# Layer 0, second MLP of a four-layer graph network: the input added inside it, sums on GpSimd, output blocks between all chunks, earlier degrees, and shorter rare branches

## The chip, the cores and the metric

The kernel runs on one core of a Trainium2 chip, as one launch. The metric is the device time of the whole program in microseconds (us). The program is a long one: some 33,600 instructions over four layers, and the change touches mostly one part of the first layer, some 340 us long, and four branches elsewhere.

## The reference

There are T = 1250 nodes with D = 512 features, and 20,000 directed edges (`src`, `dst`). Each of four layers adds to x a graph convolution and a mixer, and then a feed-forward part with experts. Layer 0 is the one that matters here:

```python
edge_index = jnp.stack([src, dst])
xn = _layernorm(x, axis=-1)
x = x + _L0_gnn_ref(xn, edge_index, ...) + _L0_mix_ref(xn[None], ...)[0]
x = x + _L0_ffn_ref(_layernorm(x, axis=-1)[None], ...)[0]

def _L0_gnn_ref(x, edge_index, W, b):          # with a loop at every node
    deg = segment_sum(ones, row); dis = rsqrt(deg)
    h = x @ W.T + b
    return relu(segment_sum((dis[row] * dis[col])[:, None] * h[row], col))

def _L0_mix_ref(x, ...):                       # two layers of attention + MLP
    for i in range(2):
        ...                                    # attention on layernorm(x), added to x
        y = layernorm(x, ln2_g[i], ln2_b[i])
        h = gelu(y @ W1[i] + b1[i])            # 512 -> 2048
        x = x + h @ W2[i] + b2[i]              # 2048 -> 512
    return x
```

## The kernel before

**Layout.** The nodes are ten tiles of 125 rows. A tensor with nodes on partitions is `[125, 10, 512]`; transposed tensors (`yT`, `hT`) have features on partitions, and the nodes are then cut into three chunks of 500, 500 and 250 columns (`CH`). All of it is in 32-bit floats. Every matmul group goes through `mm` (L187), or through L1181 in the products described next. PSUM results are taken by DVE or ACT; `add_to` (L213) adds a PSUM result into a tile on DVE. The scheduler keeps an engine's instructions in an order that follows the program's; `tc.keep_in_program_order` and `pinned` fix an instruction or a load at its place.

**The MLP of layer 0.** `l0_mlp(i, ...)` runs over four units u (512 hidden features each) and, within a unit, over the three chunks. A product of two matrices is made as seven products of quarter blocks (`seven`) in place of eight: before it, sums and differences of the quarters are formed, by `left_sums` (L1163 to L1166) and `right_sums` (L1170 to L1173), and while it runs, intermediate results are copied out of PSUM to `p` by ACT (L1185), combined on DVE (L1194, L1195), and added to the outputs. `hidden` makes `hT` of one chunk from `yT`, the first weights and `tx`, the sums of the chunk's quarters of `yT`. `outputs` makes the output rows of one chunk from `hT` and the second weights, two node tiles (a block) at a time, and adds each quarter into `xm` (which is `xn` here) on DVE: L1311 adds an earlier result out of SBUF, L213 one out of PSUM. In unit 1 the bias `b2` is added to each finished tile (L1328).

The first MLP is called with `roomy=True`: `tx` has room for all chunks and is made once. The second MLP, the one of the change, is not roomy, because the graph's tensors need space. There `tx` is a single buffer that is made anew on DVE for every chunk of every unit, as soon as the hidden products before it are done with it. The order of its blocks is written out: hidden of chunk 0, hidden of chunk 1, outputs of chunk 0, hidden of chunk 2, outputs of chunk 1, outputs of chunk 2, and then the next unit.

**Work aside.** After each of the twelve chunks, the second MLP calls `aside()`, which runs one piece of the generator `steps()`: five pieces with two calls of `graph.arrived(t)`, five with the scaling of two tiles of `hs` by `dis` and its division into two parts (`parted`, L678 and L679), and then `graph.degrees()`. The graph is a matrix of counts of 1250x1250, made earlier in DRAM (`adj`). `arrived(t)` loads 125 rows of it by a DMA of GpSimd's queue into `at`, sums the rows on DVE (L643, into `degO`), and adds them into `self.into` on GpSimd (L647). `degrees()` sums over the partitions by matmuls, once as a column for each tile (`degI`) and once as rows (`ps<-at,ones`), takes the inverse of the rows on DVE (L665, L666), writes it to DRAM (`inv_row`), and sets the flag `heavy`, which says whether a node has more than 4096 edges.

**The graph convolution.** After the MLP, the `Columns` object fetches the counts in five pieces of 250 columns (1.22 MB each, SyncE's queue), the first two or three ahead, and between them x is loaded again (five loads, 2.56 MB), and the weights of the shared expert. Then `l0_gnn` goes over the ten tiles: twenty matmuls gather the tile (`ps<-hs,AT`), DVE adds `hs`, ACT takes the relu, DVE adds it to x (L870), GpSimd adds `xn` (L871), and `arrival[0].step(t)` makes the layer norm (L486 to L491), the transposes and the gate logits (`gw`) of what follows.

**Rare branches.** Where a count is over 4096, the fast matmuls need a second part. `over` holds this: a value of `heavy` is loaded, and `with tc.If(some > 0)` (L749) runs the additional products. It stands in all four layers and isn't taken with these inputs. All engines take part in the branch, and each engine's body must be jumped over. The feed-forward parts have a similar branch in `Experts.run` (the list of assignments being longer than usual), which isn't taken either.

**Queues.** Loads of weights, of x and of the columns share SyncE's queue (SP), which works in order. GpSimd (POOL) issues the loads of the counts itself.

Of the kernel before, what the change touches and what calls it, by code (L numbers as in the profile page):

```python
# [8 lines left out]
F32 = mybir.dt.float32  # L9
# [15 lines left out]
E = 8  # L25
# [32 lines left out]
def gps_d4_kernel(ctx: ExitStack, tc: tile.TileContext, a: dict, out: bass.AP):  # L58
# [23 lines left out]
    def load_x(engine, o, pinned=False, between=lambda pinned: None):  # L82
        for t in range(0, NT, 2):
            move(engine, o[:, t:t + 2, :], a["x"][t * TP:(t + 2) * TP, :].rearrange("(t p) d -> p t d", p=TP), pinned)
            if t in (0, 4):
                between(pinned=True)
# [273 lines left out]
    class Experts:  # L360
# [101 lines left out]
    class Arrival:  # L462
# [3 lines left out]
        def __init__(self, n, gate, xT=None, hidden=None):  # L466
# [5 lines left out]
            self.gw = pool.tile([P, self.k, E], F32, name="gw")  # L472
            nc.sync.dma_start(self.gw, gate.rearrange("(c p) e -> p c e", p=P))
            self.xT, self.hidden = xT, hidden
            self.ps = bank()
            self.turned = None
# [76 lines left out]
    class Graph:  # L553
# [84 lines left out]
        def arrived(self, t):  # L638

            order = tc.keep_in_program_order  # L640
            at = self.at
            move(nc.gpsimd, at, adj[t * TP * T:(t + 1) * TP * T, :].rearrange("(p d) o -> p (d o)", d=T))
            order(nc.vector.tensor_reduce(degO[:, t:t + 1], at, AX.X, OP.add))  # L643
            if t == 0:
                nc.gpsimd.tensor_copy(self.into, at)
            else:
                nc.gpsimd.tensor_tensor(self.into, self.into, at, op=OP.add)  # L647
# [61 lines left out]
    class Columns:  # L709
# [35 lines left out]
    def over(use, rows=None, xn=None, given=None):  # L745


        some = nc.values_load(heavy[0:1, 0:1], min_val=0, max_val=1)
        with tc.If(some > 0):  # L749
            W = 500 if rows is None else TP  # L750
            with tc.tile_pool(name="over", bufs=1) as pool:
                more = [given(pool)] if given is not None else []

                def rest(s, c0, cn):
                    at = pool.tile([TP, W], F32, tag="at", name="at")
                    nc.sync.dma_start(at[:, :cn], counts()[:, s, c0:c0 + cn])
                    hi = pool.tile([TP, W], I32, tag="hi", name="hi")
                    nc.vector.tensor_scalar(hi[:, :cn], at[:, :cn].bitcast(I32), -4096, None, op0=OP.bitwise_and)
                    lo = pool.tile([TP, W], F32R, tag="lo", name="lo")
                    nc.vector.tensor_tensor(lo[:, :cn], at[:, :cn], hi[:, :cn].bitcast(F32), op=OP.subtract)  # L760
                    return lo

                def flags(s, k):
                    return dict(start=(s == 0 and k == 0), stop=(s == NT - 1 and k == 1))

                if rows is not None:
                    for d in range(NT):
                        ps = bank()
                        for s in range(NT):
                            lo = rest(s, d * TP, TP)  # L770
                            for k in range(2):
                                nc.tensor.matmul(ps[:TP, :], lo, rows[:, s, k, :], **flags(s, k))
                        use(d, ps[:TP, :])
                for c0, cn in CH if rows is None else []:
                    for f in range(NC):
                        part = part_feature(pool, xn, f, "part")
                        ps = bank()
                        for s in range(NT):
                            lo = rest(s, c0, cn)
                            for k in range(2):  # L780
                                nc.tensor.matmul(ps[:, :cn], part[:, s, k, :], lo[:, :cn], **flags(s, k))
                        use(f, c0, cn, ps[:, :cn], *more)
# [80 lines left out]
    def l0_gnn(columns, rows, dis, hs, xn):  # L863
        over(lambda d, ps: add_to(hs[:, d, :], ps), rows=rows)
        for t in range(NT):
# [4 lines left out]
            nc.vector.tensor_tensor(x[:, t, :], x[:, t, :], u, op=OP.add)  # L870
            nc.gpsimd.tensor_tensor(x[:, t, :], x[:, t, :], xn[:, t, :], op=OP.add)  # L871
# [296 lines left out]
    def right_sums(o, b11, b12, b21, b22, last=None):  # L1168
        v = nc.vector
# [35 lines left out]
    def l0_mlp(i, xm, yT, front, then=None, aside=lambda: None, roomy=True):  # L1205
# [3 lines left out]
        with tc.tile_pool(name=f"mlp{i}", bufs=1) as mp:  # L1209
            tx = mp.tile([P, 4, 2, T // 2], F32, name="tx") if roomy else None  # L1210
# [22 lines left out]
            def sums(u, c0, cn):  # L1233
# [5 lines left out]
                if u == 0 or not roomy:  # L1239
                    right_sums(t, yT[:, 0:2, left], yT[:, 0:2, right], yT[:, 2:4, left], yT[:, 2:4, right], t[:, 3])  # L1240
# [56 lines left out]
            def outputs(unit, c0, cn, hT):  # L1297
# [4 lines left out]
                for j in range(n // TP):  # L1302
# [64 lines left out]
            if roomy:  # L1367
                outputs(*before)

    def layer0_mixers():  # L1370
# [3 lines left out]
        with tc.tile_pool(name="l0a", bufs=1) as pool:  # L1374
# [16 lines left out]
            with tc.tile_pool(name="gnn", bufs=1) as gp:  # L1391
                rows = gp.tile([TP, NT, 2, D], F32R, name="hs2")
                dis = S.small.tile([TP, NT], F32, tag="dis", name="dis")
                with tc.tile_pool(name="columns", bufs=1) as cp:
                    graph.fetch(cp)

                    def steps():
# [4 lines left out]
                        inv_sqrt_deg(degO, dis)  # L1402
                        for t in range(NT):
# [816 lines left out]
```

## Time and profile before

| | us |
|---|---|
| three runs | 3005.89, 3014.81, 3008.05 |
| median | 3008.05 |
| the profiled execution, its own time | 3007.94 |
| its span (first to last instruction) | 3006.2 |
| TensorE busy | 2753.6 (92%) |
| DVE busy | 1421.4 (47%) |
| ACT busy | 763.0 (25%) |
| GpSimd busy | 673.0 (22%) |
| mean granted TensorE clock | 0.952 |

In the profile, PE is TensorE's matmul, PEld its weight load, DVE is VectorE, ACT is ScalarE, POOL is GpSimd, and SP is SyncE. Each row of a group or a timeline names the line of the kernel, the engine, the operation, the tiles (out<-in), the shapes, and in brackets the idle time of the engine before it with what released it ("<-DVE xn L213": the result of line 213 on DVE; "DVEq" is DVE's own instruction queue, such as a branch). A busy share is an average over stages with different limits, so the stage around the change has to be read by itself.

### The profile page before, as it was taken

To read this page: it belongs to the slowest core of one execution; us is meant where nothing else is said; L and a number is where in the kernel's file an instruction comes from. 1 tells how busy PE (TensorE), PEld (TensorE's weight loads), DVE (VectorE), ACT (ScalarE), POOL (GpSimd) and SP (SyncE) were. 2 spreads that over 40 slices of the span, in tenths; PEclk is the share of its full clock that TensorE was granted. 3 is DMA by queue.
4 is the path that set the end of the run, shared out by engine and by line. 5 is a ranking of instruction groups with operands and counts; after the bars stand their busy time and mean duration, and the time that the engine had idled before them with its cause. 6 is when DMAs were issued, how large, how long until landed. Compare 5 with 4: busy or idle time off the path is not lost. (4 is left out here: it accounts for less than half of the span.)

```text
span 3006.2 us, 33629 instructions
## 1 busy us (share of the span) xinstructions
PE 2753.6 (92%) x12041; PEld 1876.9 (62%) x12041; DVE 1421.4 (47%) x3477; ACT 763.0 (25%) x1715; POOL 673.0 (22%) x496
## 2 busy tenths in 40 slices
PE   7999999999999999889999978999799998889893
PEld 4457778865586878656475556667454657545562
DVE  6835677673356887444541550000324135443523
ACT  3233333342233333120211531111131022320010
POOL 3444444444000300042310001000201002032123
PEclk9999999999999999899999988999899998999897
DMA  8411112111000210638620018775340016651296
GB/s 238 122 15 15 3 29 47 29 33 15 15 15 24 87 45 15 161 108 263 164 77 1 21 35 300 249 239 195 94 132 15 1 35 207 204 145 44 61 317 196
DMA packets 248445, 301.59 MB, mean 100 GB/s; under 512 B 105258, under 2 KB 142509, under 8 KB 248247
## 3 DMA queue, kind: packets, MB, share of 16 engines
q1 hardware_dynamic: 137303, 208.28, 22.2%
q0 software_dynamic: 97408, 66.17, 9.7%
q10 hardware_dynamic: 13536, 24.65, 2.2%
q8 instruction: 106, 1.74, 0.2%
q14 instruction: 92, 0.75, 0.1%
HBM read 253.68 MB, written 44.91 MB: 99 GB/s over the span
## 5 line engine op out<-in xcount | busy, mean ns | idle before, releaser
L627 POOL DMA_INDIRECT adj<-count,cell x160 | 323.7, 2023 | 356.6 <-DMA adj<-count,cell 319.7
L187 PE MATMUL ps<-xnT,w 128*128 128x500 f32 (+1 forms) x832 | 311.7, 528 | 4.0 <-DVEq L749 3.3
L187 PE MATMUL ps<-w,hT 128*128 128x512 f32 (+1 forms) x592 | 264.7, 596 | 3.8 <-ACT hT L1504 3.8
L187 PE MATMUL ps<-w,xnT 128*125 128x512 f32 x560 | 251.5, 598 | 1.5 <-ACT xnT L1657 1.5
L187 PEld LDWEIGHTS ps<-xnT,w 128*128 128x128 f32 x832 | 158.2, 193 | 143.6 <-issue 133.2
L187 PE MATMUL ps<-xgT,w 128*128 128x256 f32 (+1 forms) x1256 | 235.8, 346 | 2.6 <-issue 1.8
L187 PEld LDWEIGHTS ps<-xgT,w 128*128 128x128 f32 x1256 | 208.8, 194 | 44.7 <-issue 19.9
L383 POOL DMA_INDIRECT xg<-rows,r_idx x94 | 89.5, 952 | 561.0 <-PE ps L424 300.5
L187 PEld LDWEIGHTS ps<-w,hT 128*128 128x128 f32 (+1 forms) x592 | 109.5, 190 | 125.3 <-issue 116.5
L425 DVE COPY xgT<-ps 128x512 f32<-128x512 f32 x94 | 61.9, 686 | 253.4 <-PE ps L424 253.4
L187 PEld LDWEIGHTS ps<-w,xnT 128*125 128x125 f32 x560 | 102.0, 189 | 115.0 <-issue 112.2
L444 POOL DMA_INDIRECT came<-yd,slots x80 | 100.1, 1252 | 294.7 <-ACT one L453 101.4
L434 DVE TENSOR_TENSOR y<-ps,erow 128x512 f32<-128x512 f32 x71 | 49.1, 691 | 199.3 <-PE ps L187 192.5
L1185 ACT COPY p<-ps 125x256 f32<-125x256 f32 (+2 forms) x252 | 86.9, 348 | 220.3 <-PE ps L1181 203.7
L1181 PE MATMUL ps<-w,hT 128*125 128x256 f32 x480 | 118.5, 380 | 1.0 <-ACT p L1185 1.0
L213 DVE TENSOR_TENSOR xn<-ps,xn 125x256 f32<-125x256 f32 (+1 forms) x180 | 79.6, 448 | 77.7 <-PE ps L187 55.5
L1805 ACT ACTIVATE hT<-ps,b 128x256 f32<-128x256 f32 (+1 forms) x112 | 48.8, 435 | 262.6 <-PE ps L187 247.8
L187 PE MATMUL ps<-hs,AT 125*125 125x512 f32 x400 | 104.6, 419 | 9.4 <-DVEq L749 9.4
L1181 PEld LDWEIGHTS ps<-w,hT 128*125 128x125 f32 x480 | 88.8, 188 | 14.3 <-ACT p L1185 1.8
L187 PEld LDWEIGHTS ps<-hs,AT 125*125 125x125 f32 x400 | 77.8, 198 | 29.6 <-DVEq L749 10.1
L187 PE MATMUL ps<-AT,part 125*128 125x500 f32 (+1 forms) x480 | 92.5, 355 | 0.0
L187 PEld LDWEIGHTS ps<-AT,part 125*128 125x128 f32 x480 | 79.4, 189 | 13.3 <-issue 0.8
(449 smaller groups left out, 4814.2 us busy)
## 6 DMA issues: line engine op xcount, KB each, us to landing
w<-in_L_ffn_we_dram SPq DMA_DIRECT2D x56, 1024.0 KB
w<-in_L_ffn_w_dram SPq DMA_DIRECT2D x58, 512.0 KB
yd<-y ACTq DMA_DIRECT2D x94, 256.0 KB
w<-in_L_mix_W_dram SPq DMA_DIRECT2D x16, 1024.0 KB
w<-in_L_ffn_w_dram SPq DMA_DIRECT2D x44, 256.0 KB
AT<-adj SPq DMA_DIRECT2D x20, 546.9 KB
rows<-z SPq DMA_DIRECT2D x40, 224.0 KB
keyrow<-keys SPq DMA_DIRECT2D x16, 546.9 KB
```

The source lines that it names most:

```text
L187: nc.tensor.matmul(o, l, r, start=(i == 0), stop=(i == n - 1))
L213: nc.vector.tensor_tensor(dst, ps, dst, op=OP.add)
L383: nc.gpsimd.indirect_dma_start(g, None, self.rows, bass.IndirectOffsetOnAxis(ap=self.idx[:, t:t + 1], axis=0))
L425: nc.vector.tensor_copy(xgT[:, :, j * SL:(j + 1) * SL], ps.rearrange("p (c s) -> p c s", c=NC))
L434: nc.vector.tensor_tensor(y, ps, bias, op=OP.add)
L444: nc.gpsimd.indirect_dma_start(y, None, yd, bass.IndirectOffsetOnAxis(ap=slots[n][:, k * NT + t:k * NT + t + 1], axis=0))
L627: nc.gpsimd.indirect_dma_start(adj, bass.IndirectOffsetOnAxis(ap=self.cell[:, c:c + 1], axis=0), self.count[:, c:c + 1], None, compute_op= ...
L1181: nc.tensor.matmul(banks[b], ls(k), rs(k), start=first and k == 0, stop=k == 1, skip_group_check=True)
L1185: nc.scalar.copy(o, banks[b])
L1805: nc.scalar.activation(hT[f // NC][:, f % NC, :ns], ps[:, :ns], AF.Gelu, bias=b1[:, f:f + 1])
```

## The change

In `l0_mlp`, for the MLP that is not roomy: the sums of a chunk's inputs go to GpSimd; x is loaded tile by tile into one buffer, `b2` is added to it and the sum is added to `xm`, both on GpSimd, in unit 1; and the outputs of the chunk before follow every chunk's hidden products, so that outputs of chunk 2 now follow hidden of the next unit's chunk 0. `degO` is made by ACT, as the sum that goes with a copy of `at` onto itself. `degrees()` moves before the scaling of `hs`, and makes the inverses from a transpose of `degI` (one reciprocal of 10x125 in place of three of one partition). The first columns are fetched right behind it, the gate weight `gw` ahead of the MLP, and x isn't loaded after the MLP any more: `l0_gnn` makes it as `xn + u`, since `xn` holds x already. `over` comes before the columns' second pool. In all layers its value is loaded once, its body is shorter, and the flag `preferred_fallthrough_block=False` lays the untaken path right behind the compare; the same flag stands at the branch of the experts.

```diff
@@ Experts.run
-            with tc.If(used > self.often + NPAIR):
+            with tc.If(used > self.often + NPAIR, preferred_fallthrough_block=False):
@@ Graph.arrived
-            order(nc.vector.tensor_reduce(degO[:, t:t + 1], at, AX.X, OP.add))
+            order(nc.scalar.activation(at, at, AF.Copy, accum_out=degO[:, t:t + 1]))
@@ Graph.degrees
-            for c0, cn in CH:
-                ps = bank()
-                mm(ps[:1, :cn], [(ones[:TP, 0:1], self.into[:, c0:c0 + cn])])
-                inv = S.small.tile([1, 500], F32, tag="inv", name="inv", bufs=1)
-                nc.vector.tensor_scalar(inv[:, :cn], ps[:1, :cn], 1.0, None, op0=OP.max)
-                nc.vector.reciprocal(inv[:, :cn], inv[:, :cn])
-                nc.sync.dma_start(inv_row[:, c0:c0 + cn], inv[:, :cn])
+            ps = bank()
+            nc.tensor.transpose(ps[:NT, :TP], degI, ident[:TP, :TP])
+            inv = S.small.tile([NT, TP], F32, tag="inv", name="inv", bufs=1)
+            nc.vector.tensor_scalar(inv, ps[:NT, :TP], 1.0, None, op0=OP.max)
+            nc.vector.reciprocal(inv, inv)
+            nc.sync.dma_start(inv_row.rearrange("o (t p) -> (o t) p", p=TP), inv)
@@ Columns.fetch
-                pool, bufs = (self.first, 1) if self.first and not self.got else (self.pool, 2)
+                pool, bufs = (self.first, 1) if self.first and len(self.got) % 3 == 0 else (self.pool, 2)
@@ over
-        some = nc.values_load(heavy[0:1, 0:1], min_val=0, max_val=1)
-        with tc.If(some > 0):
+        if "some" not in soon:
+            soon["some"] = nc.values_load(heavy[0:1, 0:1], min_val=0, max_val=1)
+        with tc.If(soon["some"] > 0, preferred_fallthrough_block=False):
...
@@ l0_gnn
-        over(lambda d, ps: add_to(hs[:, d, :], ps), rows=rows)
...
-            nc.vector.tensor_tensor(x[:, t, :], x[:, t, :], u, op=OP.add)
-            nc.gpsimd.tensor_tensor(x[:, t, :], x[:, t, :], xn[:, t, :], op=OP.add)
+            nc.vector.tensor_tensor(x[:, t, :], xn[:, t, :], u, op=OP.add)
@@ right_sums
-    def right_sums(o, b11, b12, b21, b22, last=None):
-        v = nc.vector
+    def right_sums(o, b11, b12, b21, b22, last=None, v=nc.vector):
@@ l0_mlp
+            beside = nc.vector if roomy else nc.gpsimd
...
-                    right_sums(t, yT[:, 0:2, left], yT[:, 0:2, right], yT[:, 2:4, left], yT[:, 2:4, right], t[:, 3])
+                    right_sums(t, yT[:, 0:2, left], yT[:, 0:2, right], yT[:, 2:4, left], yT[:, 2:4, right], t[:, 3],
+                               beside)
...
-                        if u == 1:
+                        if u == 1 and roomy:
                             nc.vector.tensor_tensor(xm[:, t, :], xm[:, t, :], b2[:TP, :], op=OP.add)
+                        if u == 1 and not roomy:
+                            xi = mp.tile([TP, D], F32, tag="xi", name="xi")
+                            nc.sync.dma_start(xi, a["x"][tok(t), :])
+                            tc.keep_in_program_order(nc.gpsimd.tensor_tensor(xi, xi, b2[:TP, :], op=OP.add))
+                            tc.keep_in_program_order(nc.gpsimd.tensor_tensor(xm[:, t, :], xm[:, t, :], xi, op=OP.add))
...
-                if c == 0:
+                if roomy and c == 0:
                     unit.second()
...
-                    if c:
+                    if before is not None:
                         outputs(*before)
-                    if c == len(CH) - 1:
-                        outputs(unit, c0, cn, hT)
+                    if c == 0:
+                        unit.second()
                 aside()
...
-            if roomy:
-                outputs(*before)
+            outputs(*before)
@@ layer0_mixers
                     graph.fetch(cp)
+                    columns = Columns(None, cp)
+                    gw = S.small.tile([P, NC, E], F32, tag="gw", name="gw", bufs=1)
+                    nc.sync.dma_start(gw, a["L0_ffn_gate_w"].rearrange("(c p) e -> p c e", p=P))
...
                         inv_sqrt_deg(degO, dis)
+                        graph.degrees()
+                        yield
+                        columns.fetch(pinned=True)
                         for t in range(NT):
...
-                        graph.degrees()
-                        yield
...
+                    over(lambda d, ps: add_to(hs[:, d, :], ps), rows=rows)
                     with tc.tile_pool(name="columns2", bufs=1) as cp2:
-                        columns = Columns(cp2, cp)
+                        columns.pool = cp2
+                        x = ctx.enter_context(tc.tile_pool(name="rows", bufs=1, side="right")).tile([TP, NT, D], F32, name="x")
                         columns.fetch(pinned=True)
-                        x = ctx.enter_context(tc.tile_pool(name="rows", bufs=1, side="right")).tile([TP, NT, D], F32, name="x")
-                        load_x(nc.sync, x, True, lambda **k: columns.fetch(**k))
+                        columns.fetch(pinned=True)
...
-                        arrival[0] = Arrival(0, a["L0_ffn_gate_w"], xnT)
+                        arrival[0] = Arrival(0, a["L0_ffn_gate_w"], xnT, gw=gw)
```

The rare body of `over` is rewritten: before, a count was loaded and divided anew for every tile or feature block; now each block of counts is loaded and divided once and serves all the matmuls that need it. On DVE the four bodies shrink from 400, 493, 493 and 401 instructions to 130, 140, 130 and 128, on SyncE (first layer) from 207 to 64; on TensorE they hold about as much work as before.

More of the change, by code (lines that the diff above doesn't have):

```diff
@@ L80, in move, with load_x @@
                 tc.keep_in_program_order(d)
-    def load_x(engine, o, pinned=False, between=lambda pinned: None):
+    def load_x(engine, o):
         for t in range(0, NT, 2):
-            move(engine, o[:, t:t + 2, :], a["x"][t * TP:(t + 2) * TP, :].rearrange("(t p) d -> p t d", p=TP), pinned)
-            if t in (0, 4):
-                between(pinned=True)
+            move(engine, o[:, t:t + 2, :], a["x"][t * TP:(t + 2) * TP, :].rearrange("(t p) d -> p t d", p=TP))
     cols = const.tile([P, NCOL], F32, name="cols")
@@ L462, in gps_d4_kernel, with __init__ @@
     class Arrival:
-        def __init__(self, n, gate, xT=None, hidden=None):
+        def __init__(self, n, gate, xT=None, hidden=None, gw=None):
             self.scope = ExitStack()
@@ L471, in __init__ @@
             self.k = gate.shape[0] // P
-            self.gw = pool.tile([P, self.k, E], F32, name="gw")
-            nc.sync.dma_start(self.gw, gate.rearrange("(c p) e -> p c e", p=P))
+            self.gw = gw
+            if gw is None:
+                self.gw = pool.tile([P, self.k, E], F32, name="gw")
+                nc.sync.dma_start(self.gw, gate.rearrange("(c p) e -> p c e", p=P))
             self.xT, self.hidden = xT, hidden
@@ L745, in over @@
     def over(use, rows=None, xn=None, given=None):
-        some = nc.values_load(heavy[0:1, 0:1], min_val=0, max_val=1)
-        with tc.If(some > 0):
-            W = 500 if rows is None else TP
+        if "some" not in soon:
+            soon["some"] = nc.values_load(heavy[0:1, 0:1], min_val=0, max_val=1)
+        with tc.If(soon["some"] > 0, preferred_fallthrough_block=False):
             with tc.tile_pool(name="over", bufs=1) as pool:
                 more = [given(pool)] if given is not None else []
[L754 to L782, printed above, removed]
@@ new lines, in over @@
+                exact = F32 if rows is None else F32R
+                for c0, cn in CH:
+                    ds = tiles_of(c0, cn)
+                    ps = [bank() for _ in (ds if rows is not None else range(NC))]
+                    for s in range(NT):
+                        at = pool.tile([TP, 500], F32, tag="at", name="at")
+                        nc.sync.dma_start(at[:, :cn], counts()[:, s, c0:c0 + cn])
+                        hi = pool.tile([TP, 500], I32, tag="hi", name="hi")
+                        nc.vector.tensor_scalar(hi[:, :cn], at[:, :cn].bitcast(I32), -4096, None, op0=OP.bitwise_and)
+                        lo = pool.tile([TP, 500], exact, tag="lo", name="lo")
+                        nc.vector.tensor_tensor(lo[:, :cn], at[:, :cn], hi[:, :cn].bitcast(F32), op=OP.subtract)
+                        if rows is None:
+                            for f in range(NC):
+                                nc.tensor.matmul(ps[f][:, :cn], xn[:, s, fea(f)], lo[:, :cn], start=s == 0, stop=s == NT - 1)
+                            continue
+                        for k in range(2):
+                            for (_, o), b in zip(ds, ps):
+                                nc.tensor.matmul(b[:TP, :], lo[:, o:o + TP], rows[:, s, k, :],
+                                                 start=s == 0 and k == 0, stop=s == NT - 1 and k == 1)
+                    if rows is None:
+                        for f in range(NC):
+                            use(f, c0, cn, ps[f][:, :cn], *more)
+                    else:
+                        for (d, _), b in zip(ds, ps):
+                            use(d, b[:TP, :])
```

## The prediction

> **What bounds the kernel now.** I read the busy times first:
>
> ```profile
> PE 2753.6 (92%) x12041; PEld 1876.9 (62%) x12041; DVE 1421.4 (47%) x3477; ACT 763.0 (25%) x1715; POOL 673.0 (22%) x496
> ```
>
> TensorE works for 92% of the span, and the change leaves nearly all matmuls in place. So its worth is the idle time of PE that it removes, less what it adds. Chain and waits of the whole program say little of this stage, so I took the windows of the second MLP (957.6 to 1222.3 us, units 0 to 3 in turn) and of the gather behind it; columns: length, then busy time and count per engine, granted clock, DMA share, GB/s.
>
> ```profile
> 945.00:1030.00 85.00, 80.80 (x381) 61.63 (x380) 69.93 (x145) 26.52 (x64) 18.57 (x17) 1.00 0.24 74
> 1030.00:1110.00 80.00, 73.17 (x361) 62.60 (x360) 71.06 (x144) 31.64 (x73) 16.92 (x13) 1.00 0.21 66
> 1110.00:1220.00 110.00, 108.72 (x567) 95.14 (x566) 86.02 (x198) 41.07 (x100) 0.00 (x0) 1.00 0.07 21
> 1220.00:1240.00 20.00, 13.93 (x50) 10.24 (x48) 4.97 (x11) 1.49 (x2) 1.29 (x1) 0.83 0.90 204
> 1240.00:1280.00 40.00, 32.18 (x148) 26.59 (x149) 13.15 (x28) 8.07 (x16) 6.44 (x5) 0.87 0.68 188
> ```
>
> PE loses 11 us in the first two rows, where GpSimd (POOL) works too, 1.3 us in the third, where it does not, and much at the head of the gather. The PE timeline there (start, us, operation, idle before and its releaser):
>
> ```profile
> 1227.54 11.67 PE L187 MATMUL ps<-hs,AT 125*125 125x512 f32 x40 [5.18 <-DVEq L749]
> 1241.75 0.62 PE L193 MATMUL ps<-ident,z 125*128 125x125 f32 x4 [2.54 <-DVE z L491]
> 1242.13 6.47 PE L187 MATMUL ps<-hs,AT 125*125 125x512 f32 x20
> 1254.64 1.81 PE L187 MATMUL ps<-gw,xnT 128*125 128x8 f32 x8 [6.04 <-DMA gw<-in_L_ffn_gate_w_dram]
> ...
> 1276.24 4.89 PE L187 MATMUL ps<-hs,AT 125*125 125x512 f32 x20
> ```
>
> An unhindered tile takes 4.89 us for its 20 matmuls (last row); the first take more, and wait, while the DMA engines are 90% busy with five loads of x (2.56 MB), two weights and the columns of counts in one queue.
>
> **Gains, part by part.**
> *Gather.* Between 1222.4 and 1254.7 (32.3 us) PE did three tiles and one set of transposes: 3 x 4.89 + .65 = 15.3 us if unhindered. 17.0 us are lost: the jump behind the rare branch (5.18), x and the columns, and the gate weight at the queue's end (6.04). The change loads x inside the MLP (DMA share .07 to .24), the first column (1.22 MB) there too, and the gate weight before. Column 1 then lands some 6 us (1.22 MB at 204 GB/s) after the branch, before tile 2 needs it at +12 us; column 2 at +12, before +24. I leave 2 us of the 17 for the jump and for the first tile's chain: -15, bounds -12 to -17.
> *Tail of the gather.* The last tile's `x` add on GpSimd (L871, 1.29 us) goes out of the chain before the 4.24 us wait at 1306.79: -1.4.
> *Order of chunks.* Hidden products of one chunk start right behind those of another and wait for p copies (L1185): .67 + 1.28 + 1.28 at 1039.95, 1107.97 and 1169.71. With an output block between, ACT has 6 us of cover: -3.2, bounds -2 to -3.2.
> *Degrees.* Six matmuls `ps<-at,ones` (2.3 us together) become one transpose (.3): -2. The reciprocals 1x500 (L666, 8.2 us for three) leave DVE; they are part of the next item.
> *Relief of DVE.* It loses 28 sums of .67 and 16 of .41 (25 us), ten b2 adds of .69 (7) and ten row sums of 1.44 (14), some 46 us, and the 8 of the reciprocals. Waits of PE on DVE in the MLP sum to about 8 us (5.6 on `xn` L213, 1.8 on `sh` L1164, .4 on `hT`), and half of that sits where a GpSimd add runs: -4, bounds -1 to -7.
> *Branches.* DVE's program shrinks in the rare bodies from 400, 493, 493, 401 instructions to 130, 140, 130, 128. Its sequencer rows put 4.4, 2.75, 2.8 and 2.85 us between compare and the next instruction at these four places; at an expert branch with 128 it is .5, at bodies of 12 to 16 .2. At each, PE's next matmul was released by DVE's queue (L749); the first stands in the timeline above, the others are:
>
> ```profile
> 1598.36 4.53 PE L187 MATMUL ps<-xnT,w 128*128 128x500 f32 x5 [3.31 <-DVEq L749]
> 2386.58 3.70 PE L187 MATMUL ps<-sT,w 128*128 128x500 f32 x4 [3.36 <-DVEq L749]
> 2705.85 2.63 PE L187 MATMUL ps<-hs,AT 125*125 125x512 f32 x7 [4.26 <-DVEq L749]
> ```
>
> The first is in the gather's 15 already. The others can each give at most 2.3 (2.8 less .5): 7 together; what comes next is PE's own jump (3.45 and 3.32 us at the second and third, now under the last matmuls) and SyncE's. I take -6, bounds 0 to -7.
> Sum of gains: 15 + 1.4 + 3.2 + 2 + 4 + 6 = 31.6.
>
> **Losses.**
> *GpSimd and DVE.* The timeline of DVE, and of POOL at the same time:
>
> ```profile
> 987.70 0.42 DVE L1194 TENSOR_TENSOR p<-p,p 125x256 f32<-125x256 f32 x1
> 988.16 0.43 DVE L1311 TENSOR_TENSOR xn<-xn,p 125x256 f32<-125x256 f32 x1
> 988.56 2.56 DVE L1195 TENSOR_TENSOR p<-p,p 125x256 f32<-125x256 f32 x1
> ```
> ```profile
> 988.46 2.39 POOL L647 TENSOR_TENSOR at<-at 125x1250 f32<-125x1250 f32 x1 [3.81 <-DMA at<-adj]
> ```
>
> A DVE add with both inputs in SBUF takes .42, and 2.56 where an add of GpSimd began before it: it ends .27 us after that add. Eight of eight such DVE operations that met an L647 were held, for .9 to 2.9 us in all; DVE operations that read PSUM were not held. So GpSimd's time is not free. New there: 28 sums 128x500 at about 1.25 (estimate: L871, 125x512, 1.29), 16 of 128x250 at .65, and 20 adds for x at 1.29: 35 + 10 + 26 = 71 us, against 33 us taken off DVE for the same work. They fall where it hurts: the one buffer of sums comes free when a hidden block ends, so the four sums start with the output block, where five such DVE adds (L1311, L1194, L1311, L1195, L1311) stand before the copy that frees a bank. At 1123.99 that copy ended .24 us before PE's last product started. Four sums of 1.25 alternating with DVE delay it by 5.0, less the 2.7 of DVE's own sums: 2.3, less .24, so 2 us per 500-chunk, 7 of them (14), and about .5 for each of four 250-chunks (2). The x adds of unit 1 add up to 3.8 us to each of five blocks, of which a block's other DVE time may hide most: 0 to 15, I take 3. By another way: nine adds of 2.4 (22 us) stand now beside some 6 us of PE's waits, .28 us per us; 71 us would cost 20. Sum taken: +19, bounds +5 to +35.
>
> [...]
>
> *ACT.* The row sums of the counts (ten, 125x1250) now stand in ACT's order and wait there for a load of 3.8 us; behind them queue the p copies that PE waits for, and GpSimd's add. Bounds 0 to +8; five places have work queued ahead, so I take +2.
> *Queues.* x tiles come one at a time through one buffer by SyncE; an add that waits for its load (about 4 us) holds the sums behind it, and w loads stand behind on SyncE: 0 to +4, taken as 0, since a turn has 18 us or more for them.
> *The branch's layout.* With the common path first, an engine's jump over the rare body comes after the drain instead of before it. PE's 3.4 us fetches (at the second and third branch, and the expert branch at 2137) would then be bare: 0 to +7, taken as +2 (it replaces DVE's wait at two of the three). [...]
>
> **The sum.** -31.6 + 19 + 2 + 2 = -8.6 from the pieces. The profiled execution took 3007.94 (span 3006.2 and 1.7 around it), the median is 3008.05, so nothing is to be corrected: 3008 - 8.6, 2999.
>
> **Rivals.**
> [...] If each 500-chunk's sums cost over 4 us (DVE alternating in both blocks of a chunk) and the x adds 3 per block, the loss is 7 x 4 + 4 x 1 + 15 = 47; with gains of 31.6 and +4 of ACT and layout that is +19, 3027, and with 35 lost +7, 3015. From a loss of 28 us on (31.6 - 4) the kernel is slower. For it: eight of eight adds held. Against: DVE is freed of 46 us.
> [...] DVE has 20% free, and the sums delay only adds with slack: loss 5, ACT 0, layout 0: -27, 2981.
> *R3, the change does less than it says.* If the gather waits for the columns, not for x, it gives 6 instead of 15, and if PE's own jump takes the place of DVE's at the other branches, they give 0: gains 16.6, losses 19, so +2, 3010, no change. For it: columns 1 and 2 still start after the branch. Against: at 204 GB/s both are there in time.
>
> **How the numbers follow.** 0.3% is 9 us, what a measurement of this kernel tells from no change. The forecast itself, -3 to -17, has .42, R2 .25, R1 .18, R3 .15. The forecast stands astride the limit of faster: I give .24 of it to faster and .18 to same. Faster .24 + .25 = .49; same .18 + .09 of R3 = .27; slower .18 of R1 + .06 of R3 = .24. The range reaches from 5 below R2 (gather and relief at their upper bounds), 2976, past R1's milder case to 3022; a heavier R1 and a fuller R2 are left out. The forecast's own range is 2991 to 3005. I predict the sum, 2999.
>
> **What would show it.** Right: PE idle below 5 us between the MLP's end and the third gather tile; L643 on ACT without a wait of PE on p; hidden blocks without waits on L1185; DVE rows L1311 and L1194 of 1.3 to 1.7 us beside L1170 on POOL; PE idle in units 2 and 3, 1.3 now, grown to some 8; L749 releases under 1 us at 1598, 2386 and 2705. Wrong: no such idle in units 2 and 3 (R2), over 30 us of it in the MLP (R1), or columns still waited for (R3).

## The result, and the profile after

The changed kernel takes 3030.86 us (median of seven runs, 3024.28 to 3038.66) against 3008.33 before (seven runs, 3001.23 to 3014.81): ratio 1.0076, 95% interval 1.0057 to 1.0096. It is slower by some 22 us, where 9 us less were forecast and the range ended at 3022. The profiled execution took 3025.07 with a span of 3023.4 us, 17.2 more than the span before; it is one of the shorter runs of this kernel.

I cut both traces at the same matmuls. The stretches are in us, from the profiled executions ("r_m" is the first matmul of the experts' placement, "xg" the first transpose of gathered expert rows):

| stretch | before | after | difference | forecast |
|---|---|---|---|---|
| second MLP, first to last matmul | 264.6 | 295.5 | +30.9 | +11.8 |
| end of MLP to last gate logits (branch, gather) | 91.1 | 76.3 | -14.8 | -16.4 |
| last logits to r_m and to xg | 31.9 | 37.4 | +5.4 | 0 |
| PE's wait at the branches of layers 1, 2, 3 | 10.9 | 10.9 | 0 | -4 |
| all else, start included | 2607.7 | 2603.3 | -4.4 | 0 |

The gather went as forecast. The loss in the MLP is two and a half times its forecast, the branches gave nothing, and a stretch that the change was not meant to touch grew by 5.4. (PE reads the start 3.5 us earlier in this execution; the starts of the experiments below lie between 949.7 and 962.4, so no reading rests on it.)

Windows of the MLP after (its length is cut into four; columns as above):

```profile
953.70:1030.00 76.30, 66.44 (x302) 51.54 (x301) 54.29 (x100) 29.46 (x66) 31.67 (x29) 0.96 0.26 81
1030.00:1110.00 80.00, 66.44 (x312) 57.38 (x311) 57.88 (x99) 26.16 (x59) 45.62 (x37) 0.91 0.23 75
1110.00:1180.00 70.00, 62.39 (x300) 53.32 (x300) 50.27 (x94) 27.75 (x63) 24.95 (x20) 0.96 0.22 63
1180.00:1250.00 70.00, 67.99 (x342) 59.42 (x341) 49.32 (x113) 26.60 (x64) 7.64 (x8) 1.00 0.00 1
sum 296.30, PE 263.25 PEld 221.66 DVE 211.76 ACT 109.96 POOL 109.89; mean PE 65.81 PEld 55.41 DVE 52.94 ACT 27.49 POOL 27.47
```

The same sum over the MLP before:

```profile
sum 264.80, PE 253.16 PEld 213.21 DVE 221.60 ACT 96.97 POOL 35.49; mean PE 63.29 PEld 53.30 DVE 55.40 ACT 24.24 POOL 8.87
```

POOL is busy for 109.9 us where it was 35.5. DVE is busy for less (211.8 against 221.6), and still PE waits for it. The group of PE's matmuls in the MLP that carries most of the waits, before and after:

```profile
L1181 PE MATMUL ps<-t,hT 128*125 128x256 f32 x80 | 21.3, 389 | 5.7 <-DVE xn L213 5.6
```
```profile
L1171 PE MATMUL ps<-t,hT 128*125 128x256 f32 x72 | 21.4, 423 | 25.1 <-DVE xn L211 25.1
```

Its waits grew by 19.4 us. PE's waits for `hT`, another result of DVE (L1271), grew by 6.3, from .4 to 6.7; those for the p copies fell from 3.7 to .2. All of PE's idle time in the MLP went from 11.6 to 33.0 us, which is +21. The other 10 us are in the busy column: the same matmuls take 263.3 us in place of 253.2, and the granted clock in the first three windows is .91 to .96 where it was 1.00.

One output block of unit 2 shows both. First POOL, then DVE, then PE in the same 8 us:

```profile
1164.04 1.07 POOL L1160 TENSOR_TENSOR tx<-xnT 128x500 f32<-128x500 f32 x1 [16.25 <-PE ps L1171]
1165.07 1.69 POOL L1163 TENSOR_TENSOR tx<-xnT 128x500 f32<-128x500 f32 x1
1166.73 1.51 POOL L1161 TENSOR_TENSOR tx<-xnT,tx 128x500 f32<-128x500 f32 x1
1168.32 1.57 POOL L1162 TENSOR_TENSOR tx<-xnT,tx 128x500 f32<-128x500 f32 x1
```
```profile
1164.13 1.53 DVE L1155 TENSOR_TENSOR s<-s,w 128x512 f32<-128x512 f32 x1
1165.58 1.73 DVE L1157 TENSOR_TENSOR w<-w 128x512 f32<-128x512 f32 x1
1167.23 1.55 DVE L1156 TENSOR_TENSOR s<-w,s 128x512 f32<-128x512 f32 x1
1168.71 1.45 DVE L1184 TENSOR_TENSOR p<-p,p 125x256 f32<-125x256 f32 x1
1170.09 0.41 DVE L1303 TENSOR_TENSOR xn<-xn,p 125x256 f32<-125x256 f32 x1
```
```profile
1167.61 1.03 PE L1171 MATMUL ps<-w,sh 128*125 128x256 f32 x4
1172.42 1.13 PE L1171 MATMUL ps<-t,hT 128*125 128x256 f32 x4 [3.78 <-DVE xn L211]
```

The two engines take turns, one instruction each. Four instructions of DVE that take .68 and .42 us alone take 1.45 to 1.73, about as long as POOL's; POOL's 1.07 become 1.5 to 1.7 as well. DVE's four last 6.26 us where they would last 2.46, and the difference, 3.8, is PE's wait of 3.78. Three of the four are sums of the next unit's weights (`left_sums`), which stand in its queue ahead of the output block, and which my sum left out.

At the gather, PE's wait at the branch is .86 us where it was 5.18, and no column is waited for:

```profile
1250.64 9.58 PE L185 MATMUL ps<-hs,AT 125*125 125x512 f32 x40 [0.86 <-DVEq L748]
1261.71 0.62 PE L191 MATMUL ps<-ident,z 125*128 125x125 f32 x4 [1.48 <-issue]
```

PE's own jump over the branch took .30 us here. In `both_dve` below, with the same branch, it took 3.67 and the wait was 4.10. It is .30 to .46 in the three kernels that have the change with the sums on GpSimd, and 3.3 to 3.9 in the nine with the sums on DVE; why stays open.

At the other branches DVE's queue is no more what is waited for, and yet the waits are as long:

```profile
1616.18 5.32 PE L185 MATMUL ps<-xnT,w 128*128 128x500 f32 x8 [3.51 <-issue]
```
```profile
2404.08 8.24 PE L185 MATMUL ps<-sT,w 128*128 128x500 f32 x13 [3.75 <-issue]
```
```profile
2725.15 2.47 PE L185 MATMUL ps<-hs,AT 125*125 125x512 f32 x8 [3.68 <-issue]
```

In the sequencer rows PE's compare at the layer 1 branch begins at 1612.87, .15 us behind the drain's wait (1612.72), and takes 3.26 us. Before, it began at 1593.22, 1.8 us ahead of the last matmul's end (1595.05), took 3.45 and was over at 1596.67; from there on PE waited for DVE's jump.

Behind the logits, PE now waits at another place, and then takes longer:

```profile
1347.76 4.44 PE L185 MATMUL ps<-r_oht,r_ohl 125*128 125x27 f16 x20 [3.66 <-DVE r_ohl L335]
1352.05 11.56 PE L185 MATMUL ps<-xnT,w 128*128 128x500 f32 x24
```

The same groups before:

```profile
1336.41 0.66 PE L187 MATMUL ps<-r_oht,r_ohl 125*128 125x27 f16 x20
1336.91 8.64 PE L187 MATMUL ps<-xnT,w 128*128 128x500 f32 x24
```

The first group now keeps step with DVE, which makes its twenty inputs (L335) in 4.55 us, from 1347.40 on, and each matmul starts as one of them is done. Of the second group, the first six matmuls take 1.04 to 1.18 us each where later ones of their size take .58: there the granted clock is .51 (1352 to 1358, last section). DVE's placement instructions beside GpSimd's bias adds (L1490) are the reason for the wait:

```profile
1339.14 1.30 DVE L307 SCALAR_TENSOR_TENSOR r_q<-r_q,r_base,r_end 125x8 f32<-125x8 f32 x1
1340.37 0.22 DVE L315 TENSOR_TENSOR r_slot<-ps,r_q 125x80 f32<-125x80 f32 x1
1340.52 1.23 DVE L316 TENSOR_TENSOR r_single<-r_single,r_q 125x80 f32<-125x80 f32 x1
1341.67 1.23 DVE L343 COPY r_th<-r_end 1x8 f32<-1x8 f32 x1
```

They took .15 to .22 before; L315, which reads PSUM, still does. The ten adds of 1.2 to 1.3 us lay beside the softmax before (1310 to 1322) and lie beside the placement now (1333 to 1346). They stand on GpSimd behind a scaling of weights (L1434) that waits for `nw`, one small DVE instruction (L1427), and that instruction has moved behind the copy of the logits.

### The profile page after: what moved, and what is told of

Read it like the earlier page. It is cut to its first block, busy times and chain, and to the rows that moved or that the text cites. A ratio compares the mean times of both kernels' runs of the same rounds, so it can differ in the third digit from the quotient of the medians.

```text
span 3023.4 us, 33646 instructions
## 1 busy us (share of the span) xinstructions
PE 2754.9 (91%) x12036; PEld 1876.4 (62%) x12036; DVE 1415.0 (47%) x3409; ACT 775.9 (26%) x1735; POOL 736.0 (24%) x550
## 3 DMA queue, kind: packets, MB, share of 16 engines
q1 hardware_dynamic: 137222, 208.28, 22.2%
## 5 line engine op out<-in xcount | busy, mean ns | idle before, releaser
L1175 ACT COPY p<-ps 125x256 f32<-125x256 f32 (+2 forms) x252 | 86.5, 347 | 230.6 <-PE ps L1171 221.6
L211 DVE TENSOR_TENSOR xn<-ps,xn 125x256 f32<-125x256 f32 (+1 forms) x180 | 79.6, 450 | 83.7 <-PE ps L185 55.6
L1806 ACT ACTIVATE hT<-ps,b 128x256 f32<-128x256 f32 (+1 forms) x112 | 48.8, 435 | 262.6 <-PE ps L185 262.6
```

Of the source, the lines that this page charges most:

```text
L211: nc.vector.tensor_tensor(dst, ps, dst, op=OP.add)
L1175: nc.scalar.copy(o, banks[b])
L1806: nc.scalar.activation(hT[f // NC][:, f % NC, :ns], ps[:, :ns], AF.Gelu, bias=b1[:, f:f + 1])
```

## The experiments

Each experiment's median is held against that of the kernel before on the same chip. Theory A is the one of the prediction's losses: adds of GpSimd and of DVE hold one another up, as in the output block shown above (1164 us), where DVE's .68 and .42 us became 1.45 to 1.73; two of the expectations call this the lock. The rival B is that the order or the other moved parts did it.

**Sums back on DVE** (`sums_dve`).

```diff
-            beside = nc.vector if roomy else nc.gpsimd
+            beside = nc.vector
```

> The changed kernel with one part undone: the input sums of the second MLP on DVE again (28 of 128x500, 16 of 128x250). Theory A (adds of GpSimd and of DVE that read two SBUF operands block one another; PE then waits for DVE's copies, and works at a lower clock after each wait): the MLP, 296.3 us with the change and 264.8 before, comes to 270-280, PE's waits on L211 fall from 25 us to under 12, and the kernel is 15 to 25 us faster than with the change (3000-3010 against 3025). Theory B (not the lock but the order does it: row sums on ACT, output blocks between all chunks, and GpSimd waiting for loads of x): the MLP stays within 5 us of 296.

3008.13 us (before 3009.47; ratio 1.000, .9985 to 1.0014), so 23 us less than the changed kernel; the MLP takes 270.4, PE's waits on L211 8.0 us, and its busy time in the MLP is back at 253.2. A is borne out, and B is out as the cause of the loss: this one part undone brings the kernel back to the time of before. The MLP keeps some 6 us more than before, which the sums on GpSimd don't explain.

**The adds of x on DVE** (`x_dve`): both `nc.gpsimd.tensor_tensor` of unit 1 become `nc.vector.tensor_tensor`.

> The changed kernel with the twenty adds of unit 1 (x and b2) on DVE, the sums still on GpSimd. Theory A: GpSimd works 26 us less and holds the sums no more behind loads of x; unit 1's PE waits (1046 to 1130 us, about 15 us) halve, the MLP takes 285-290, the kernel 6-12 us less than with the change. Theory B (order): no change; if DVE is short of time in unit 1 instead, up to 5 us slower.

3030.98, MLP 296.9: no change. A's expectation of 6 to 12 us was wrong here. With twenty adds of .69 more in DVE's own time, nothing is won while the sums stay on GpSimd.

**Both on DVE** (`both_dve`).

> The changed kernel with both on DVE, so that GpSimd has only the count adds of before. Theory A: the MLP comes to 250-262, below the 264.8 of before, the gather stage keeps its 15 us, the kernel takes 2980-2992. Theory B: the MLP stays above 280 and the kernel above 3010.

3006.74, MLP 268.6. Against `sums_dve` the adds of x make 1.4 us, which these runs don't tell from nothing. The MLP did not get below the 264.6 of before, so the kernel missed the expected 2980 to 2992. PE's waits for `hT` are 7.7 us here, .4 before. Three of them, 4.8 us together, stand behind an add of DVE that waited for its load of x, such as this one:

```profile
1067.13 0.69 DVE L1324 TENSOR_TENSOR xi<-xi,row 125x512 f32<-125x512 f32 x1 [2.80 <-DMA xi<-in_x_dram]
1067.73 0.28 DVE L1271 TENSOR_TENSOR hT<-ps,p 128x125 f32<-128x125 f32 x1
```
```profile
1068.07 0.71 PE L1171 MATMUL ps<-tx,w 128*128 128x125 f32 x4 [2.50 <-DVE hT L1271]
```

So x in one buffer has a price on DVE too, of the size of the 4 us by which the MLP stays above that of before; that it is the cause is not shown, since no run here has two buffers. The three branches (9.2 us of waits) and the stretch behind the logits (36.0) are much as in the changed kernel; the experiments below take them up.

**The sums alone, put into the kernel before** (`b_sums_pool`).

```diff
-                    right_sums(t, yT[:, 0:2, left], yT[:, 0:2, right], yT[:, 2:4, left], yT[:, 2:4, right], t[:, 3])
+                    right_sums(t, yT[:, 0:2, left], yT[:, 0:2, right], yT[:, 2:4, left], yT[:, 2:4, right], t[:, 3],
+                               nc.vector if roomy else nc.gpsimd)
```

> The kernel before with one part of the change alone: the input sums of the second MLP on GpSimd. Theory A (adds of GpSimd and DVE with SBUF operands hold one another up): the MLP, 264.6 us before, grows by 15 to 25 us, PE waits on L213, and the kernel is 15 to 25 us slower than before. Rival (the sums cost only together with what else the change put beside them, loads of x and row sums on ACT): under 6 us slower.

3032.66 (before 3008.89; ratio 1.0085, 1.0053 to 1.0117), MLP 291.0. Nothing else of the change is in it, and the whole kernel loses as much as with the change (+24 us against +23), +26.4 us in the MLP. PE waits for two results there, that of DVE and that of GpSimd:

```profile
L1180 PE MATMUL ps<-tx,s 128*128 128x250 f32 (+1 forms) x176 | 36.7, 351 | 7.4 <-POOL tx L1170 7.4
...
L1180 PE MATMUL ps<-t,hT 128*125 128x256 f32 x80 | 24.3, 431 | 16.4 <-DVE xn L213 16.2
```

PE's idle time grows by 16.8 us, and its busy time by 9.4 (253.2 to 262.6).

**No flag at the counts' branch** (`noflag_over`); the short bodies stay.

```diff
-        with tc.If(soon["some"] > 0, preferred_fallthrough_block=False):
+        with tc.If(soon["some"] > 0):
```

> The changed kernel without the flag at the rare branch of the counts (the shorter body stays). Theory L (with the common path laid first, PE's own jump of 3.3 us comes after the drain and is bare): PE's waits at the branches of layers 1, 2 and 3, now 3.5, 3.75 and 3.7 us, fall to about 1 each, so 6 to 8 us less in all. Rival M (the jump of another engine, SyncE or ACT, takes its place, or PE's jump was never hidden): within 2 us of the changed kernel.

3015.69, 15 us less than the changed kernel. The waits at the three branches:

```profile
1615.62 2.75 PE L185 MATMUL ps<-xnT,w 128*128 128x500 f32 x6 [1.69 <-PEq L748]
```
```profile
2401.59 4.85 PE L185 MATMUL ps<-sT,w 128*128 128x500 f32 x11 [1.41 <-PEq L748]
```
```profile
2716.92 4.92 PE L185 MATMUL ps<-hs,AT 125*125 125x512 f32 x20 [1.69 <-DVEq L748]
```

10.9 us have become 4.8. PE's compare at layer 1 now starts at 1611.69, beside the last matmuls. So theory L holds, though the jump, 3.76 us here, still outlasts those matmuls by 1.5. The 6 us read at these waits are less than the 15 between the medians. Most of the rest stands right behind the waits: the first matmuls there run at a lower clock where the wait was long. The 32 of layer 2, before (behind a wait of 3.36 us), after (3.75) and here (1.41) (columns: length, PE busy, granted clock, DMA share, GB/s):

```profile
2386.58:2403.13 16.55, 16.55 (x32) 0.81 0.02 1
```
```profile
2404.08:2420.13 16.05, 16.05 (x32) 0.84 0.00 1
```
```profile
2401.59:2415.08 13.49, 13.49 (x32) 1.00 0.01 2
```

At layers 1, 2 and 3 the first 8, 32 and 20 matmuls take 29.7 us before, 28.0 after and 22.2 here, 5.8 less. Waits and matmuls together make 12 us of the 15; the other 3 are not traced.

**No flag, and both on DVE** (`both_noflag`).

> Sums and x adds on DVE (as in the run named both_dve, 3006.7) and no flag at either kind of branch. Theory L (the flag bares PE's own jump): 8 to 15 us less than both_dve, 2992 to 2999. Rival (the flag's cost goes over into the waits of DVE once the lock is gone): within 4 us of 3006.7.

2996.56 (before 3008.89; ratio .9949, .9926 to .9973): 10 us from the flags. In the traces, waits at the three branches fall from 9.2 us to 4.6, and the same matmuls behind them from 27.6 to 22.2, 10 us as well. **The flag at the experts' branch alone** (`flag_exp`):

> The kernel of both_noflag with the flag left at the experts' branch alone. Theory L (a far jump of PE costs 3.3 us, and of four experts' branches only the second, with 192 instructions of PE, is far): 0 to 4 us more than 2996.6. If that flag, not the one of the counts' branch, made the difference: 6 to 10 us more.

2999.44; 2.9 us more than without, but on another chip, where the kernel before is 2.9 us slower too (3011.83). So the flag at the experts' branch costs nothing that these runs show; the counts' branch made the difference.

**nw made early** (`nw_early`, on both_noflag: right behind the second MLP).

> The kernel of both_noflag with the small vector nw of layer 1 (one DVE instruction, L1427, which the change lets stand behind the logits' copy) made at the start instead, so that GpSimd's scaling of weights and its ten adds to x (L1434, L1490) run earlier. Theory P (these adds stand beside the placement in the changed kernel and hold DVE there, 15.6 us from r_oht to xg against 9.0 before): 3 to 7 us less than both_noflag, the stretch from the last logits to xg back to 32 from 36 to 37 us. Rival (PE's slow clock behind the wait, whatever DVE does, is the cause): no change.

2997.59, no gain. The part from r_oht to xg is back at 9.0 us, as said; but GpSimd's ten adds now run beside the softmax, and the stretch up to r_m grew from 7.1 to 15.9. Logits to xg are 38.6 us against 36.0. Theory P named the right instructions and the wrong remedy: wherever the adds lie on that chain, they cost.

**The old block order** (`all_order`, on nw_early).

> The kernel of nw_early with the block order of before (two hidden chunks in a row, then outputs). If the interleaved order saves PE's waits on L1175 (3.2 us before): 2 to 4 us slower than nw_early. If it instead puts the x adds and row sums where DVE is late (MLP of 268.6 with both on DVE against 264.6 before): 2 to 6 us faster.

3001.99, 4.4 us more, MLP 278.4 against 268.8. PE's waits for the p copies are 4.4 us in place of .7. The new order is worth some 4 us by the medians; the 9.6 between the two profiled MLPs are more, but they compare one of the longer runs of this kernel (3006.51) with the shortest of the other (2990.61).

**Bias adds on DVE in the gather** (`sb2_dve`), **and the row sums of the counts on DVE too** (`sb2_degO`), both on both_noflag.

```diff
             arrival[0].step(t)
+            if t == 0:
+                sb2 = row_bc(a["L0_ffn_sb2"])
+            nc.vector.tensor_tensor(x[:, t, :], x[:, t, :], sb2[:TP, :], op=OP.add)
...
-                for t in range(NT):
-                    nc.gpsimd.tensor_tensor(x[:, t, :], x[:, t, :], sb2[:TP, :], op=OP.add)
```

> The kernel of both_noflag (2996.6) with the ten adds of the shared expert's bias to x (L1490, 13 us of GpSimd beside the choice of experts) on DVE, one behind each tile's layer norm in the gather. Theory A (GpSimd's adds hold DVE there, on the chain from the logits to the first expert rows): the stretch from last logits to xg falls from 36 to about 28.5 (7.1 + 12.4 + 9.0, each the lowest seen), the gather grows by 0 to 2, so 5 to 8 us less: 2989 to 2992. Rival (that chain is set by ACT, PE and the loads, and the held DVE instructions lie beside it): within 2 us of 2996.6.

> The kernel of sb2_dve with the row sums of the counts (L643) on DVE as before. If ACT's sums cost PE waits (they stand between its p copies, and GpSimd's count add waits for them): the MLP falls from 269 to 262-266, 3 to 6 us less than sb2_dve. If they relieve DVE (14 us of it in units 0 and 1, where PE waits on DVE): 3 to 8 us more.

2985.29 and 2991.64 (before 3011.83). In both, the bias comes ahead of a layer norm that must not have it, so these two kernels don't compute the reference's result and the experts get other rows; they are held against one another only. From the logits to xg both take 26.9 us. The row sums on DVE cost 6 us, and the MLP grows from 269.3 to 277.4 (the profile of `sb2_degO`, at 3006.1, is its slowest run, so the 8 us may be too many): with all else on DVE, ACT was the right place for them.

**The bias adds a tile later** (`sb2_lag`, on both_noflag: tile t - 1 behind step t, the last one behind the last step).

> The kernel of both_noflag (2996.6) with the ten bias adds to x on DVE in the gather, each now a tile later, behind the layer norm that still needs x without the bias (in sb2_dve and sb2_degO the bias came ahead of the norm, so the experts' choice saw other values). Theory A (these adds of GpSimd, L1490, held DVE on the chain from the logits to the first expert rows): last logits to xg 26 to 29 us against 36.0, the gather as in both_noflag (78.3) or up to 2 more, 2986 to 2991. Rival (the shorter chain in sb2_dve came from the other values): within 2 us of 2996.6.

2984.43 us (before 3009.26; ratio .992, .9902 to .9938). From the logits to xg it is 26.9 us against 36.0, and PE's rows there run at full clock:

```profile
1319.64 0.66 PE L185 MATMUL ps<-r_oht,r_ohl 125*128 125x27 f16 x20
1320.15 8.64 PE L185 MATMUL ps<-xnT,w 128*128 128x500 f32 x24
```

This version beats both kernels: it is the change without the adds that it had put on GpSimd, with the bias adds out of the placement's way, and without the flag. Expected were 2986 to 2991; what it is below them lies inside the spread of its runs (2980 to 2996).

## Why the prediction was wrong, point by point

**The step that failed** is the term "2 us per 500-chunk, 7 of them (14), and about .5 for each of four 250-chunks (2)", together with the relief of DVE that stood against it. `b_sums_pool` measures the sums by themselves: 26.4 us in the MLP, for which 16 less their share of the relief was forecast. The mechanism was the right one, and R1, the first rival (over 4 us for each 500-chunk's sums), its full form; my price was too small. First, I priced waits alone: PE came back from long waits at a lower clock (four matmuls took 2.07 us behind a wait of 4.75, 1.03 later; .96 to .98 over the four windows of that MLP, 1.00 before), and PE's busy time grew by 9.4 of the 26.4. Second, the 16.8 us of idle time come close to the 16, but partly by luck: 7.4 of them are waits for GpSimd's sums themselves, which the term does not hold, and no relief came off. In the changed kernel, where the order gives the sums time and PE doesn't wait for them, the waits for DVE alone grew by 24 us, from 7.8 to 32.1. There I had let the sums of GpSimd hold only the five adds of the output block, and left out that DVE's own sums of weights and of hT stand ahead of them and take turns too, three of the four held instructions in the block shown. And I took 1.25 us for a sum, while under turns it is 1.5 to 1.7, so four last 5.9 us, not 5.0; the block's wait is 3.78 where the term has 2. My second way, .28 us per us of GpSimd, counted waits alone as well: it gives 13 us for 45 us of sums, and 26.4 is .59 per us.

**Relief of DVE** (-4) was not there for the sums: DVE's busy time fell by 9.8 us, where 54 had been taken off it, and what it gave away it paid back in longer instructions. For the row sums it was there: with the sums on DVE, having them on ACT saves 6 us.

**The x adds** (+3): on GpSimd they cost 0 to 1.4 us more than on DVE. What they cost in either place is not measured by itself; on DVE their loads make 4.8 us of PE's waits. **ACT's row sums** (+2): the price on ACT's side was not there, PE's waits for p fell to .2 us. **The order of chunks** (-3.2) gives some 4. **The gather with its tail** (-16.4) gives 14.8, within its bounds, and by the mechanism named: x and the gate weight gone from the queue, the columns there in time. Two things were luck or misread. PE's own jump took .30 us in this kernel; in the six runs with the sums on DVE and no bias adds in the gather it took 3.3 to 3.9, and the stretch is 78.7 to 82.8 us, a gain of 8 to 12. And part of what I put down to the loads was the clock: the first forty matmuls took 11.67 us before, at a clock of .80, and 9.58 after, at 1.00, with the DMA engines moving 235 and 204 GB/s.

**Branches.** The two terms (-6 for the bodies, +2 for the layout) were to be of unlike size and came out alike. Without the flag the bodies are worth 6 us at the three waits, as forecast, and 7.5 more in the matmuls right behind them, which the term does not hold; with it, PE's jump of 3.3 us is bare at each of the three, so the layout costs 12 in the traces (10 to 15 by the medians). That the jump sets the wait shows in `both_dve` too: at the third branch its jump took .40 us, and PE waited 1.69. I had bounded it at 7 and then taken 2, on the argument that it would only replace DVE's wait; it replaced it with one just as long. What fills PE's jump no run shows; its length is what was measured, 3.26 to 3.33 us at these three. That is the half of R3 that came true, PE's own jump in DVE's place.

**Not priced at all** was the stretch behind the logits (+5.4). The change moves one DVE instruction there past the logits' copy, and so 13 us of GpSimd adds to a place where DVE's placement is on PE's path.

For the MLP's adds my rows gave 19 us (the sums and bias adds taken off DVE make 32 us by the prediction's own counts, not 33). The runs show 26.4 for the sums alone, 16.8 of it waits, and 30.9 for the whole MLP. In the block shown, DVE's four instructions last 1.45 to 1.73 us beside GpSimd's of 1.07 to 1.69.

R1 at 35 us lost gave 3015 and at 47 us 3027; the profiled execution is at 3025 and the median at 3031. R1 comes out near partly for another reason: it kept gains of 31.6, of which the 6 of the branches and the sums' part of the relief did not come. The chance of .24 for slower was too low, since the eight held instructions already said that GpSimd's time adds to DVE's.

## What to carry to other kernels

Before moving two-operand adds from DVE to GpSimd, count how many DVE instructions with SBUF operands stand in its queue at that time, and give each of them one GpSimd instruction more (in the block shown four of them took 6.26 us in place of 2.46); if a copy that PE waits for stands behind them, DVE has won nothing (PE waited 3.78 us there). ACT is another matter: in the changed kernel a row sum of 1.25 us at 1022.02 stood beside DVE adds (L1303) of .43, and in `sb2_dve` the row sums on ACT saved 6 us. The shorter rare branch was worth its time only where the engine that is next late, here PE with its own jump of 3.3 to 3.8 us, could make part of that jump under the work before the drain: PE then waited 1.4 to 1.7 us (`noflag_over`), and 3.5 to 3.75 where it could not.

## What the runs showed of the hardware that was not expected

A wait can cost PE more than its length. Behind the wait of 6.25 us in unit 0, four matmuls took 2.07 us in place of 1.03 to 1.13, and behind the 3.66 us at r_oht the clock stood at half (columns: PE busy, granted clock, DMA share, GB/s):

```profile
1344.00:1348.00 4.00, 0.32 (x3) 0.96 0.00 0
1348.00:1352.00 4.00, 3.70 (x18) 0.50 0.68 188
1352.00:1358.00 6.00, 6.00 (x9) 0.51 0.85 254
1358.00:1364.00 6.00, 6.00 (x24) 1.00 1.01 355
```

Ten microseconds at half the clock follow a wait of under four. But the length alone does not decide what follows. In `b_sums_pool` the same eight matmuls stand twice behind a wait of 3.09 us:

```profile
1118.54 1.96 PE L1180 MATMUL ps<-tx,s 128*128 128x250 f32 x8 [3.09 <-POOL tx L1170]
```
```profile
1188.87 3.60 PE L1180 MATMUL ps<-tx,s 128*128 128x250 f32 x8 [3.09 <-POOL tx L1170]
```

The granted clock over the four microseconds from there is 1.00 the first time and .58 the second. A wait of 3.69 us (in `sums_dve`, layer 2) left the 32 matmuls behind it at 13.65 us and a clock of 1.00, and one of 2.31 (in `both_noflag`, layer 3, `w,totb`) was followed by a clock of .68. Behind the waits of 3.6 us and more in the changed kernel's MLP (3.60, 3.78, 3.79, 4.86 and 6.25) the clock of the next four microseconds was .50 to .65, and behind the 3.66 at r_oht .50; behind one of 2.18 in that MLP it was 1.00. What decides between equal waits stays open.

Small instructions are held in full. A copy of eight numbers on one partition (L343) took 1.23 us beside GpSimd's adds of 1.30 and .15 without them. GpSimd's scaling of weights (L1434) held DVE far less: beside its 6.3 us one DVE instruction (L229) took .70 us where .24 is usual, and none of the others took more than .34.
